# Depthwise taps of a convolution-attention kernel: the second row group's matrix products leave TensorE, and VectorE's taps are placed anew in the first image's dense stage

## Chip, cores and metric

The kernel runs on one core of a Trainium2 chip. The core has a matrix engine (TensorE, PE in the profile, with PEld for its weight loads), VectorE (DVE), ScalarE (ACT), GpSimd (POOL) and SyncE (SP); the last two mainly issue DMAs here. Each engine runs its own instructions in order and waits for others by semaphores. The metric is device time in microseconds (us), the median of several runs. All times inside the program are counted from the start of the profiled execution's span.

## What is computed

Four images of 384 channels by 48x48 pixels go through one layer. It has a depthwise 7x7 convolution (49 taps per channel) whose normalised result is added to the queries of an eight-head attention over 2304 tokens, an output projection and a residual:

```python
local = lax.conv_general_dilated(x, conv_w, window_strides=(1, 1), padding='SAME',
    dimension_numbers=('NCHW', 'OIHW', 'NCHW'), feature_group_count=C)
local = local * inv[None, :, None, None] + (bn_beta - bn_mean * inv)[None, :, None, None]
x_norm = _layernorm(x_flat, ln_gamma, ln_beta)
qkv = x_norm @ qkv_w.T + qkv_b
local_q = _layernorm(local_flat, ln_gamma, ln_beta)
q = q + local_q
attn = jax.nn.softmax(jnp.einsum('bhnd,bhmd->bhnm', q, k) * scale, axis=-1)
out = x_flat + (attn @ v) @ proj_w.T + proj_b
```

## The kernel before

**Tiles.** Channels lie on 128 partitions in three chunks. An image's 48 rows are cut into five row groups of 8, 10, 10, 10 and 10 rows (384 or 480 columns). The code counts these over all images as t = 0 to 19. Keys and values are made by six column groups of 384 tokens (g = 0 to 5).

**Dense stage of the first image.** Group g = 0 is made first, then a loop runs over g = 1 to 5 (inside the main function, after `making = from_x(0, 0)`). For each g, `from_x` yields projections on TensorE (line L568): values, keys, queries. Between its steps the loop writes the layer norm of the next group: `mean_by_chunk` (TensorE), `centre` (VectorE, L489), `squares` (ScalarE), `mean_by_chunk` of the squares, `root` (ScalarE), `newton` and `scale` (VectorE, L505, L506, L563). The scaled group is what the next group's projections read. `lows_out(n)` writes n low halves of keys on VectorE (L661) and sends keys out by DMA (`keys_out`): pair 0 on SP into the key stacks, the others on GpSimd into a DRAM tile `wide`. In the last pass (g = 5) the norm is that of row group 0's convolution, and it ends in `query_end(0)`, `high_queries(0, 0)` and `low_queries(0, 0)`. Those make the first pair's queries; `low_queries` ends in six DMAs on SP (L830, L832), which stack them for the score matmuls.

**Attention slots.** After that each row group has 12 slots: pairs of heads p = 0 to 3 times three thirds of the keys. A slot has six score tiles (L952, each followed by an exponential on ScalarE, L960) and then six weighing steps (L967). The tile `pt` that an exponential writes is shared, four buffers in all, with the dense stage's key tiles `k`, so it waits for their DMAs. At a pair's second slot `high_queries` (ScalarE) and `low_queries` (VectorE, L825, then SP's DMAs) make the next pair's queries. For the first four row groups of an image, the next row group's convolution is normalised by means on TensorE: for row group 0 after its slot 8 TensorE takes the mean of row group 1's sums, so it needs all of their taps.

**Taps.** `conv_ops(t)` yields one VectorE instruction per tap and chunk (L307; the first tap of a chunk L303), 147 in all per row group, into the sums `acc`. Taps are ordered by distance from the centre and go over the chunks in turn. For the first two row groups some taps of chunk 0 are done on TensorE instead: `products` multiplies the slab of pixels by diagonal matrices made on ScalarE. Row group 0 has 10 such taps (`PE_TAPS`), row group 1 has 18 (`MORE_TAPS`); the remaining taps of chunk 0 then come after all those of chunks 1 and 2. The 18 diagonals are made by `make_more` (L335) in two `qs` buffers, and the products are issued after the dense loop, as the last work of TensorE before slot 0; ScalarE writes their sum to the accumulator (L1105).

**Where taps run.** In the dense stage `convolve_first(n)` issues the next n taps at the place where it stands. From slot 0 on `convolve(point)` issues a share. `plan` fixes the shares before anything runs: each half slot has an estimated spare VectorE time (`room`), each row group's convolution has a place by which it is due (`due`), and the taps at a place are its room times the highest rate that any of the coming due places asks for.

**Order.** On PE, VectorE and ScalarE the order is that of the code. The order of the DMA issues on SP and GpSimd is chosen by a scheduler.

Of the kernel before, what the change touches and what calls it, by code (L numbers as in the profile page):

```python
# [10 lines left out]
F32 = mybir.dt.float32  # L11
HALF = mybir.dt.float32r
AF = mybir.ActivationFunctionType
# [3 lines left out]
P = 128  # L17
# [12 lines left out]
OUT_SLOT = 7  # L30
WARM = 14
PE_TAPS = 10
MORE_TAPS = 18

# [11 lines left out]
def unshifted_pass(  # L48
# [16 lines left out]
    nc = tc.nc  # L65
# [3 lines left out]
    CC = C // P  # L69
# [10 lines left out]
    GM = max(ROWS) * W  # L80
# [5 lines left out]
    def size(a):  # L86
        return a.stop - a.start

    def columns_of(t):
        return size(tokens[t % NA])  # L90
# [3 lines left out]
    work = ctx.enter_context(tc.tile_pool(name="work", bufs=2))  # L94
# [5 lines left out]
    def two_banks(name="r"):  # L100
        return ps.tile([P, 2, 512], F32, tag="r", name=name)
# [19 lines left out]
    slabs = {}  # L121

    def load_slab(b, g, parts=1, queue=nc.gpsimd):
        first, end = max(0, row_of[g] - PAD), min(H, row_of[g + 1] + PAD)
        t = work.tile([P, CC, GM + 2 * PAD * W], F32, tag="slab", name=f"slab{b}_{g}")

        edges = (first, row_of[g + 1], end) if parts == 2 else (first, end)
        for a, e in zip(edges, edges[1:]):
            load_packed(t[:, :, (a - first) * W : (e - first) * W], x[b, :, a * W : e * W], queue)
        slabs[b, g] = (t, first, end)  # L130
# [15 lines left out]
    cw, shift = vec[:, :, 0:T0], vec[:, :, T0]  # L146
# [7 lines left out]
    ident = const.tile([P, P], F32, tag="ident", name="ident")  # L154
# [46 lines left out]
    for c in range(CC):  # L201
        for r, n, first in ((0, HD, 0), (64, HD, 1), (48, 16, 6), (112, 16, 7)):
            head = first + 2 * c if first < 6 else first
            ch = head * HD + (16 * c if first >= 6 else 0)
            while n:
                part = min(n, P - ch % P)
                pieces.append((c, r, ch // P, ch % P, part))
                r, n, ch = r + part, n - part, ch + part
# [56 lines left out]
    taps = sorted(range(KS * KS), key=lambda t: (abs(t // KS - PAD), abs(t % KS - PAD)))  # L265
    accs = {}

    def window(slab, a, g, first, end, c, tap):

        dy, dx = tap // KS - PAD, tap % KS - PAD  # L270
        r0, r1 = max(row_of[g], -dy), min(row_of[g + 1], H - dy)
        c0, c1 = max(0, -dx), min(W, W - dx)
        if r0 >= r1:
            return None
        img = slab[:, c, : (end - first) * W].rearrange("p (h w) -> p h w", w=W)
        a = a.rearrange("p (h w) -> p h w", w=W)
        return (
            img[:, r0 + dy - first : r1 + dy - first, c0 + dx : c1 + dx],
            a[:, r0 - row_of[g] : r1 - row_of[g], c0:c1],
        )  # L280

    def conv_ops(t):
        b, g = divmod(t, NA)
        if t + 1 < NT:
            load_slab(*divmod(t + 1, NA))
        slab, first, end = slabs[b, g]
        acc = work.tile([P, CC, GM], F32, tag="acc", name=f"acc{t}", bufs=3)[:, :, : columns_of(t)]
        accs[t] = acc
        if t == 0:
            nc.vector.memset(acc[:, 0, :], 0.0)  # L290

        order = [(tap, c) for tap in taps for c in range(CC)]
        if t < 2:
            mine = [(tap, 0) for tap in taps[(PE_TAPS, MORE_TAPS)[t] :]]
            order = [o for o in order if o[1]] + mine
        for tap, c in order:
            part = window(slab, acc[:, c, :], g, first, end, c, tap)
            if not part:
                continue
            src, dst = part  # L300
            weight = cw[:, c, tap : tap + 1]
            if tap == taps[0]:
                nc.vector.tensor_scalar(  # L303
                    dst, src, weight, shift[:, c : c + 1], ALU.mult, ALU.add
                )
            else:
                nc.vector.scalar_tensor_tensor(dst, src, weight, dst, ALU.mult, ALU.add)  # L307
            yield

    def diagonal(i):  # L310
        return diagonals[i // 6].rearrange("p i f -> p (i f)")[:, i % 6 * P : i % 6 * P + P]
# [2 lines left out]
        for i in range(PE_TAPS):  # L314
            nc.scalar.mul(diagonal(i), ident, cw[:, 0, taps[i] : taps[i] + 1])

    def products(g, n, diagonal):
        total = two_banks()[:, 0, : columns_of(g)]
        slab, first, end = slabs[0, g]
        for i, tap in enumerate(taps[:n]):  # L320
            src, part = window(slab, total, g, first, end, 0, tap)
            nc.tensor.matmul(part, lhsT=diagonal(i), rhs=src, start=i == 0, stop=i == n - 1)  # L322
        return total

    more = []

    def more_diagonal(i):
        return more[i // 9][:, i % 9 * P : i % 9 * P + P]

    def make_more():  # L330
        for tag, bufs in (("qs", 5), ("qs", 5)):
            d = work.tile([P, CC, GM], F32, tag=tag, name="more", bufs=bufs)
            more.append(d.rearrange("p c g -> p (c g)"))
            for i in range(9 * len(more) - 9, 9 * len(more)):
                nc.scalar.mul(more_diagonal(i), ident, cw[:, 0, taps[i] : taps[i] + 1])  # L335
            yield

# [41 lines left out]
            (5, 1): 4.5, (5, 2): 0.6,  # L381
        }.get((g, h), 0.0)

    points, room = [], []
    for t in range(NT):
        if t % NA == 0 and t:
            points += [("kv", t, g, h) for g in range(NG) for h in range(5)]
# [3 lines left out]
    each = CC * KS * KS  # L391
    due = []
    counts = [0]
    weights = [0.0]
    for t in range(1, NT):
        last = ("slot", t - 1, norm_slots(t - 1)[0] - (t >= NA), t < NA) if t % NA else ("kv", t, 4, 0)
        counts.append(t * each - MORE_TAPS)
        weights.append(weights[-1] + (counts[-1] - counts[-2]) * columns_of(t) / G)
        due.append((points.index(last), weights[-1]))
    share = {}  # L400
# [6 lines left out]
    def plan(done):  # L407

        given = done
        done = done * columns_of(1) / G  # L410
        for i, point in enumerate(points):
            ahead = [(sum(room[i:end]), n - done) for end, n in due if end > i]
            rate = max((n / time for time, n in ahead[: 2 * NA]), default=0.0)
            done += rate * room[i]
            share[point] = taps_in_all(done) - given
            given = taps_in_all(done)
        assert given == counts[-1]

    def convolve(*point):
        for _ in range(share[point]):  # L420
            next(stream)
# [6 lines left out]
    class Norm:  # L428
# [34 lines left out]
        def sum(self):  # L463
            self.add(self.src)
# [239 lines left out]
    def lows_out(n):  # L704
        for _ in range(n):
            lows.popleft()()
# [63 lines left out]
    def key_bias(m):  # L770
        nc.vector.tensor_add(qkb[:, 1, :], qk_vec[:, 1, :], m[1])
        nc.vector.tensor_add(vbp[:, :, 0], vbp[:, :, 0], m[2])

    def query_bias(m):

        nc.vector.tensor_add(qkb[:, 0, :], qk_vec[:, 0, :], m[0])
        nc.vector.tensor_add(qkb[:, 0, :], qkb[:, 0, :], beta)
# [218 lines left out]
    def convolve_first(n):  # L996
        nonlocal n_first
        n_first += n
        for _ in range(n):
            next(stream)  # L1000
# [36 lines left out]
    next(making)  # L1037
    for c in range(CC):
        scale_rows(0, c)
    first_sum = products(0, PE_TAPS, diagonal)  # L1040
    m, bank = columns()
    convolve_first(10)
    norm = Norm(xn[0, 1])
    norm.mean_by_chunk(norm.src, bank)
    convolve_first(12)
    key_bias(m)
    query_bias(m)
    next(making)
    norm.centre()
# [9 lines left out]
    norm.scale(norm.newton())  # L1059
    both(making)  # L1060
    convolve_first(7)
    making_more = make_more()
    for g in range(1, NG):

        last = g == NG - 1
        next(making_more, None)
        making = from_x(0, g)
        both(making)
        assert not last or n_first >= each - PE_TAPS
        norm = Norm(accs[0] if last else xn[0, g + 1])  # L1070
        norm.mean_by_chunk(norm.src)
        if last:
            added = output_bias()
        if g in (3, 5):
            keep_stack(0, g // 2 - 1)
        convolve_first(4)
        norm.centre()
        norm.squares()
        both(making)
        if not last:  # L1080
            convolve_first(4)
            both(making)
        norm.mean_by_chunk(norm.buf)
        norm.root()
        lows_out(1)
        if last:
            both(making)
        both(making)
        convolve_first(6 if last else 10)
        if not last:  # L1090
            lows_out(2)
        if last:
            local_end(0, norm.newton())
        else:
            norm.scale(norm.newton())
        next(making)
        if last:
            query_end(0)
            high_queries(0, 0)
            low_queries(0, 0)  # L1100
        next(making)
        if not last:
            convolve_first(7)
    lows_out(2)
    nc.scalar.activation(  # L1105
        accs[1][:, 0, :], products(1, MORE_TAPS, more_diagonal), AF.Identity, bias=shift[:, 0:1]
    )
    nc.vector.tensor_add(pb, pb, added)
    plan(n_first - (each - PE_TAPS))

    for t in range(NT):
        b, g = divmod(t, NA)
# [71 lines left out]
        first, second = norm_slots(t)  # L1184
        for s in range(NSLOT):
            pair, part = divmod(s, KB // BATCH)
# [90 lines left out]
    for i, at in enumerate(pieces_out):  # L1277
        ao, n = aos[i], size(at)
# [555 lines left out]
```

## Time and profile before

| what | value |
|---|---|
| median of 4 runs | 2785.94 us (2783.3 to 2787.38) |
| the profiled execution's own time | 2785.26 us |
| its span, first to last instruction | 2783.5 us |
| PE busy | 2750.2 us (99%) |
| DVE busy | 2340.1 us (84%) |
| ACT busy | 1639.5 us (59%) |
| POOL busy | 696.1 us (25%) |
| taps on VectorE, L307, 2854 instructions | 1679.5 us |
| products with diagonals of row group 1, L322, on the chain | 14.05 us, from 158.31 us |
| first score matmul | 172.29 us |
| mean granted TensorE clock | 0.996 of full speed |

A busy engine in the profile is not necessarily one at full speed, since the ends of matmuls are modelled. A row of a timeline gives start, length, engine, line, operation, output and inputs, shapes and count; the bracket at its end is the engine's idle time before it and what ended that.

### The profile page before, as it was taken

How to read it: one execution, taken by the hardware profiler on the slowest of the kernel's cores; microseconds unless marked ns; L12 is line 12 of the kernel's file. 1: busy time of each engine (PE TensorE's matmuls, PEld its weight loads, DVE VectorE, ACT ScalarE, POOL GpSimd, SP SyncE). 2: the span in 40 equal slices, each digit the busy share in tenths (PEclk: the TensorE clock that was granted, in tenths of full speed). 3: DMA queues.
4: the chain of work that ended last, by engine and by line, in shares of the span. 5: the costliest groups of instructions: out<-in, count | busy, mean ns of one | idle time of the engine just before them, and what ended most of it. 6: DMA issues, size and time to landing. Idle time of an engine off the chain costs nothing.

```text
span 2783.5 us, 46399 instructions
## 1 busy us (share of the span) xinstructions
PE 2750.2 (99%) x16438; PEld 1556.8 (56%) x16438; DVE 2340.1 (84%) x4082; ACT 1639.5 (59%) x2281; POOL 696.1 (25%) x1273
## 2 busy tenths in 40 slices
PE   9998999999999999999999999999999999999999
PEld 6565555555555655555556565555555565555555
DVE  6879999989999999989888999898889889987112
ACT  4345666666423766767632577677652276676662
POOL 5731111111375111110257311101117701110110
PEclk9999999999999999999999999999999999999999
DMA  7344444445455454454635554545546545444442
GB/s 142 98 113 122 121 123 131 121 127 134 126 165 151 130 140 129 129 143 124 167 104 153 151 145 127 126 126 148 135 121 167 128 141 133 138 125 137 141 145 75
DMA packets 163298, 369.15 MB, mean 133 GB/s; under 512 B 61488, under 2 KB 112208, under 8 KB 163056
## 3 DMA queue, kind: packets, MB, share of 16 engines
q0 software_dynamic: 76992, 284.75, 35.9%
q1 hardware_dynamic: 83072, 77.72, 12.3%
q10 hardware_dynamic: 2992, 3.62, 0.4%
q8 instruction: 132, 2.16, 0.3%
q14 instruction: 110, 0.90, 0.1%
HBM read 258.14 MB, written 64.14 MB: 116 GB/s over the span
## 4 chain that ended last, share of the span: by engine, by line
PE 88%; DVE 7%; POOL 2%; DMA 2%; ACT 1%; issue 1%; SPq 0%; DVEq 0%; ACTq 0%; POOLq 0%
PE o L967 39%; PE r L952 31%; PE r L568 16%; DVE acc L307 5%; DMA wide<-k 1%; PE r L322 1%; POOL wide L594 1%; DMA slab<-in_x_dram 1%; POOL wide L619 0%; POOL wide L592 0%; POOL wide L591 0%; POOL wide L613 0%; DMA qs<-qs 0%; DVE k L661 0%; PE r L1010 0%
## 5 line engine op out<-in xcount | busy, mean ns | idle before, releaser
L307 DVE SCALAR_TENSOR_TENSOR acc<-slab,vec,acc 128x450 f32<-128x450 f32 (+8 forms) x2854 | 1679.5, 657 | 2.2
L960 ACT ACTIVATE pt<-r 128x960 f32<-128x960 f32 (+1 forms) x1440 | 1248.5, 943 | 237.6 <-PE o L967 150.0
L967 PE MATMUL o<-pt,v 128*64 128x480 f32 (+1 forms) x5760 | 1169.7, 556 | 5.6 <-ACT pt L960 5.6
L952 PE MATMUL r<-qs,ks 64*128 64x480 f32 (+1 forms) x8640 | 969.3, 373 | 9.6 <-DMA qs<-qs 6.4
L952 PEld LDWEIGHTS r<-qs,ks 64*128 64x128 f32 x8640 | 784.0, 184 | 276.9 <-issue 167.9
L967 PEld LDWEIGHTS o<-pt,v 128*64 128x64 f32 x5760 | 394.2, 137 | 665.9 <-issue 584.7
L628 POOL DMA_DIRECT2D ks<-wide x228 | 165.5, 726 | 1363.5 <-PE r L952 1323.1
L568 PE MATMUL r<-xn,w_qk 128*128 128x384 f32 x864 | 283.7, 486 | 0.0
L849 ACT COPY o<-o 113x480 f32<-113x480 f32 (+1 forms) x160 | 87.1, 544 | 299.4 <-PE o L967 299.4
L568 PEld LDWEIGHTS r<-xn,w_qk 128*128 128x128 f32 x864 | 164.3, 190 | 114.3
L868 DVE TENSOR_TENSOR ao<-ao,o 113x480 f32<-113x480 f32 (+1 forms) x120 | 76.1, 634 | 97.1 <-ACT o L849 97.0
L568 PE MATMUL r<-w_v,xn 128*128 128x384 f32 x432 | 144.7, 487 | 0.0
L650 ACT COPY v<-r 128x384 f32<-128x384 f32 x72 | 32.1, 480 | 188.4 <-PE r L568 188.4
L568 PEld LDWEIGHTS r<-w_v,xn 128*128 128x128 f32 x432 | 81.6, 190 | 58.1 <-issue 2.9
L594 POOL DMA_DIRECT2D wide<-k x192 | 96.5, 507 | 10.4 <-issue 7.4
L619 POOL DMA_DIRECT2D wide<-k x192 | 93.0, 489 | 0.1
L859 ACT COPY ao<-o 113x480 f32<-113x480 f32 (+1 forms) x60 | 32.7, 545 | 102.1 <-PE o L967 102.1
L613 POOL DMA_DIRECT2D wide<-k x144 | 71.7, 500 | 77.4 <-ACT k L658 60.6
L825 DVE TENSOR_TENSOR qs<-xn,qs 128x480 fp32r<-128x480 f32 (+1 forms) x60 | 38.0, 633 | 57.4 <-ACT qs L820 57.3
L108 POOL DMA_DIRECT2D slab<-in_x_dram x76 | 47.1, 626 | 155.0 <-DVE acc L307 154.7
L568 PE MATMUL r<-af,w_o 128*128 128x384 f32 (+1 forms) x270 | 85.2, 470 | 0.0
L675 ACT ACTIVATE xn<-r,qkb 128x384 f32<-128x384 f32 x72 | 41.2, 578 | 67.4 <-PE r L568 65.6
(139 smaller groups left out, 1349.2 us busy)
## 6 DMA issues: line engine op xcount, KB each, us to landing
ks<-wide POOLq DMA_DIRECT2D x228, 768.0 KB, 5.2
qs<-qs SPq DMA_DIRECT2D x352, 60.0 KB
wide<-k POOLq DMA_DIRECT2D x480, 24.0 KB, 1.9
slab<-in_x_dram POOLq DMA_DIRECT2D x24, 432.0 KB, 7.2
wide<-k POOLq DMA_DIRECT2D x192, 48.0 KB, 1.9
wide<-ks POOLq DMA_DIRECT2D x12, 768.0 KB, 4.2
xr<-in_x_dram POOLq DMA_DIRECT2D x16, 576.0 KB, 5.5
rb<-rden SPq DMA_DIRECT2D x32, 270.0 KB
```

What stands on the lines that cost most here:

```text
L108: queue.dma_start(out=dst[p0 : p0 + piece.shape[0]], in_=piece)
L307: nc.vector.scalar_tensor_tensor(dst, src, weight, dst, ALU.mult, ALU.add)
L568: nc.tensor.matmul(dst, lhsT=weights(c), rhs=src(c), start=c == 0, stop=c == CC - 1)
L594: queue.dma_start(out=dst[r + 32 * i : r + 32 * i + 32, 1], in_=k[r + 16 : r + HD, 1])
L613: nc.gpsimd.dma_start(out=last[16 * u : 16 * u + 16, 0], in_=k[r : r + 16, 0])
L619: nc.gpsimd.dma_start(out=last[to : to + 16, 1], in_=k[r : r + 16, 1])
L628: nc.gpsimd.dma_start(out=place_keys(b, p, i), in_=wide[b, p][:, :, at])
L849: nc.scalar.copy(part[0 : 64 + HA], sums[0 : 64 + HA, 0, :n])
L868: nc.vector.tensor_add(dst, dst, part[0 : 64 + HA])
L952: nc.tensor.matmul(r[:, j, :n], lhsT=ks[rows, w, at], rhs=qs[rows, m, :], start=i == 0, stop=i == 2,)
L960: nc.scalar.activation(pt, r[:, :, :n], AF.Exp, scale=SCALE)
L967: nc.tensor.matmul(sums[halves[j], 0, : columns_of(t)], lhsT=values[t // NA, kb // NB][:, first : first + 64], rhs=pt[:, j, :], start=i == ...
```

## The change

`MORE_TAPS` and everything that served it go: the 18 products of row group 1, the two tiles of diagonals with their 18 ScalarE instructions, and the ScalarE copy of the sum. Row group 1 is convolved wholly on VectorE, its 147 taps in the common order over three chunks. In the dense stage the numbers of taps at the places change: 46 instead of 37 ahead of the loop, 32 instead of 25 in each of the passes g = 1 to 4, 21 instead of 10 in the last pass, which has a new place behind `root`. The planner gets a new place, `("start",)`, with a room of 14.0 us ahead of slot 0, and its share is issued there.

```diff
-MORE_TAPS = 18
+FIRST_ROOM = 14.0
...
-        if t < 2:
-            mine = [(tap, 0) for tap in taps[(PE_TAPS, MORE_TAPS)[t] :]]
-            order = [o for o in order if o[1]] + mine
+        if t == 0:
+            order = [o for o in order if o[1]] + [(tap, 0) for tap in taps[PE_TAPS:]]
...
-    def make_more():
-        for tag, bufs in (("qs", 5), ("qs", 5)):
-            d = work.tile([P, CC, GM], F32, tag=tag, name="more", bufs=bufs)
-            more.append(d.rearrange("p c g -> p (c g)"))
-            for i in range(9 * len(more) - 9, 9 * len(more)):
-                nc.scalar.mul(more_diagonal(i), ident, cw[:, 0, taps[i] : taps[i] + 1])
-            yield
...
-    points, room = [], []
+    points, room = [("start",)], [FIRST_ROOM]
...
-        counts.append(t * each - MORE_TAPS)
+        counts.append(t * each)
...
     norm.mean_by_chunk(norm.src, bank)
-    convolve_first(12)
+    convolve_first(18)
     key_bias(m)
+    convolve_first(3)
     query_bias(m)
...
     for g in range(1, NG):
...
-        next(making_more, None)
...
-        convolve_first(4)
+        convolve_first(8)
         norm.centre()
         norm.squares()
         both(making)
         if not last:
-            convolve_first(4)
+            convolve_first(7)
             both(making)
         norm.mean_by_chunk(norm.buf)
         norm.root()
+        if last:
+            convolve_first(9)
         lows_out(1)
...
-        convolve_first(6 if last else 10)
+        convolve_first(4 if last else 10)
...
     lows_out(2)
-    nc.scalar.activation(
-        accs[1][:, 0, :], products(1, MORE_TAPS, more_diagonal), AF.Identity, bias=shift[:, 0:1]
-    )
     nc.vector.tensor_add(pb, pb, added)
     plan(n_first - (each - PE_TAPS))
+    convolve("start")
```

More of the change, by code (lines that the diff above doesn't have):

```diff
@@ L315, in make_diagonals, with products @@
             nc.scalar.mul(diagonal(i), ident, cw[:, 0, taps[i] : taps[i] + 1])
[L317 to L322, printed above, removed]
-        return total
-    more = []
-    def more_diagonal(i):
-        return more[i // 9][:, i % 9 * P : i % 9 * P + P]
-    def make_more():
-        for tag, bufs in (("qs", 5), ("qs", 5)):
-            d = work.tile([P, CC, GM], F32, tag=tag, name="more", bufs=bufs)
-            more.append(d.rearrange("p c g -> p (c g)"))
-            for i in range(9 * len(more) - 9, 9 * len(more)):
-                nc.scalar.mul(more_diagonal(i), ident, cw[:, 0, taps[i] : taps[i] + 1])
-            yield
+    def products():
+        total = two_banks()[:, 0, : columns_of(0)]
+        slab, first, end = slabs[0, 0]
+        for i, tap in enumerate(taps[:PE_TAPS]):
+            src, part = window(slab, total, 0, first, end, 0, tap)
+            nc.tensor.matmul(
+                part, lhsT=diagonal(i), rhs=src, start=i == 0, stop=i == PE_TAPS - 1
+            )
+        return total
     def norm_slots(t):
@@ L1039, in unshifted_pass @@
         scale_rows(0, c)
-    first_sum = products(0, PE_TAPS, diagonal)
+    first_sum = products()
     m, bank = columns()
@@ L1061, in unshifted_pass @@
     convolve_first(7)
-    making_more = make_more()
     for g in range(1, NG):
         last = g == NG - 1
-        next(making_more, None)
         making = from_x(0, g)
```

## The prediction

> **What bounds the kernel now.** The change touches only the first image, so I read the chain of waits up to 380 us first. It shows TensorE without a gap through the dense stage, then row group 1's products, then slot 0:
>
> ```profile
> 36.13 122.18 PE r L568 x390
> 158.31 14.05 PE r L322 x36
> 172.36 3.35 PE r L952 x36
> ```
>
> Next TensorE's timeline over the first row group's slots, whose idle times are in the brackets:
>
> ```profile
> 235.56 4.09 PE L967 MATMUL o<-pt,v 128*64 128x384 f32 x24
> 247.50 5.14 PE L568 MATMUL r<-acc,mean_w 128*128 128x480 f32 x6 [7.85 <-DVE acc L307]
> ...
> 281.63 4.18 PE L952 MATMUL r<-qs,ks 64*128 64x480 f32 x35 [2.17 <-DMA qs<-qs]
> ```
>
> After slot 8 TensorE waits 7.85 us for row group 1's last tap, and the six matmuls then take 5.14 us where the same shape takes 2.68 at 260.14 us. The windows by stage show why, in the clock column (0.74):
>
> ```profile
> 240.00:260.00 20.00, 12.50 (x66) 6.78 (x66) 19.38 (x31) 6.57 (x11) 3.79 (x6) 0.74 0.56 120
> ```
>
> So VectorE's taps cost 7.85 + 2.46 = 10.3 us here. VectorE's own timeline tells where it could have worked earlier:
>
> ```profile
> 77.00 1.35 DVE L489 TENSOR_TENSOR xn<-xn,r 128x1152 f32<-128x1152 f32 x1 [2.28 <-PE r L568]
> ...
> 81.86 0.62 DVE L661 SCALAR_TENSOR_TENSOR k<-r,qkb,k 128x384 fp32r<-128x384 f32 x1 [1.49 <-ACT k L658]
> ...
> 131.86 0.61 DVE L505 SCALAR_TENSOR_TENSOR sq<-r,eps,sq 128x384 f32<-128x384 f32 x1
> ...
> 147.73 0.62 DVE L661 SCALAR_TENSOR_TENSOR k<-r,qkb,k 128x384 fp32r<-128x384 f32 x1 [5.52 <-DMA slab<-in_x_dram]
> ...
> 157.75 12.99 DVE L307 SCALAR_TENSOR_TENSOR acc<-slab,vec,acc 128x450 f32<-128x450 f32 x21
> 180.71 0.56 DVE L825 TENSOR_TENSOR qs<-xn,qs 128x384 fp32r<-128x384 f32 x1 [9.98 <-ACT qs L820]
> ```
>
> It idles some 4 us a pass up to g = 3, less at g = 4, 5.52 in the last pass and 9.98 before slot 1's queries.
>
> **Removed.** 14.05 us of TensorE. ScalarE's 18 diagonals (5.5 us busy) and one copy (0.66 us) lie beside idle time of ScalarE and are worth nothing.
>
> **Added to VectorE.** 18 taps, but the remaining ones get cheaper. The same shapes cost less when neighbours write different chunks:
>
> ```profile
> 199.26 8.57 DVE L307 SCALAR_TENSOR_TENSOR acc<-slab,vec,acc 128x460 f32<-128x460 f32 x14
> ...
> 237.84 9.51 DVE L307 SCALAR_TENSOR_TENSOR acc<-slab,vec,acc 128x480 f32<-128x480 f32 x13
> ```
>
> 8.57/14 = 0.61 us with two chunks in turn, 9.51/13 = 0.73 with chunk 0 alone. Before: 98 x 0.61 + 31 x 0.73 = 82.4 us; after: 147 x 0.61 = 89.7, so +7.3 us. [...]
>
> **The dense stage gets longer.** A pass takes TensorE 21.28 us (L489 waited for it at 55.72, 77.00 and 98.28). VectorE's fixed work per pass is 1.27 (L489) + 3 x 0.53 (L661) + 2.52 (L505, L506, L563) = 5.4 us, which leaves 15.9 for taps. After the change 32 lie between one pass's L505 and the next's. Adding up the start-to-start steps of the same taps where they now stand (row group 1's at 0.61): taps 72 to 103 take 15.1 us, 104 to 135 (chunk 0 alone) 18.6, 136 to 167 19.3. So VectorE overruns by 2.7 us in g = 3 and 3.4 in g = 4; with 0.5 late at g = 2 its `newton` is 6.6 us late at g = 4. TensorE's next group begins at 70.99 and 21.28-us steps after, 1.25 us behind the end of `scale` (69.74). The rest, 5.3 us, is TensorE's delay, and with 0.2 for late squares in the last pass the stage ends at 163.8 instead of 158.3.
>
> Last pass: `scale` of g = 4 ends at 140.1; 15 taps 9.2, centre 1.4, 9 taps 5.5, one low 0.5, 4 taps 2.4, `newton` to `query_end` 4.2, `low_queries` 0.6: 163.8 (156.7 before), the two lows at 164.3 and 164.8.
>
> **Slot 0: the cover is gone.** The 14 us also hid what comes behind `low_queries`: SP's six DMAs and the key DMAs on GpSimd, which must land before the third exponential may overwrite a shared `pt` buffer. The second image's start, which has no products, shows both waits (TensorE, then ScalarE):
>
> ```profile
> 878.25 3.82 PE L952 MATMUL r<-qs,ks 64*128 64x384 f32 x35 [1.43 <-DMA qs<-qs]
> 884.01 5.79 PE L967 MATMUL o<-pt,v 128*64 128x384 f32 x24 [1.94 <-ACT pt L960]
> ```
> ```profile
> 883.06 0.81 ACT L960 ACTIVATE pt<-r 128x768 f32<-128x768 f32 x1 [2.17 <-DMA wide<-k]
> ```
>
> There the exponential came 9.1 us after the second low (873.97). In the first image's own rows GpSimd issued that tile's last DMA at 163.4 after a low at 157.2, plus 0.5 to issue and 2.0 to land, less 0.5 for an issue that moves ahead: 8.2 us. So the third exponential starts at 172.5 to 173.9, weighing 0.95 later, lasting 4.1 or (as at 884.01) 5.8 us. Slot 1 starts at 177.4 to 180.6, against 179.67 before. I take 179.0: of the 14 us removed, 0.7 is left.
>
> The Trainium skill, TensorE: Matmul & The Clock Gate, section "Why this matters for your kernels", speaks against the change: TensorE idle for more than about 3 us falls back to half clock. Between 163.8 and the queries' landing it would idle some 4 us; by the rule one window of about 3.4 us at half rate, 1.7 us, most of it under the wait for the exponential. The row at 884.01 has the same 1.7 us after 1.43 and 1.94 us of idling, the row at 281.63 nothing after 2.17.
>
> **Ahead of slot 0, and a new wait.** By the planner's arithmetic the start gets 24 taps, row group 0's slots 123 (153 before). Pair 1's `low_queries` now stands behind 24 + 16 taps: 164.9 + 24.5 + 0.6 = 190.0. Behind it wait SP's four DMAs, and TensorE's slot 3. From such a low to its scores took 6.8 us (274.79 to 281.63, one key load beside it) and 9.5 us (208.30 to 217.84, image loads too); the first is nearer, I take 7: 197.0. Undisturbed, slot 3 would start at 179.0 + 2 x 7.38 = 193.8; TensorE waits 3.2 us. Pair 2: 33 taps 20.2 and three short instructions 1.4 later, 211.6, landed at 218.6 to 221.1, against slot 6 at 197.0 + 22.1 = 219.1: 1 us more, 220.1 (217.84 before). Pair 3 is free of it (233 against 242). Row group 1's last tap ends 16 taps later, 222; TensorE asks at 220.1 + 22.1 = 242.2. The 7.85 and the 2.46 are gone: the mean ends at 244.9 instead of 252.56, 7.7 us. One tap fewer ahead of `low_queries(1, 0)` gives 0.6 of the 2.17, the earlier taps 0.2 at 354.55; half clock after the new waits takes 0.5 back. Sum 8 us. From 380 us on TensorE hardly waits and the plan nearly repeats, so it is kept: 2785.26 - 8 = 2777.3, and 2778 beside the median, which lies 0.7 above the profiled execution.
>
> **Rivals.** *Full gain:* the taps fit the waits, the queries land in time: 14.05 + 10.3 = 24, so 2762. For it: the idle brackets. Against it: 18.6 and 19.3 us of taps in 15.9 of room, and the second image's start. Chance 0.08. *Moved, not paid:* the waits at slots 3 and 6 eat what slot 8 gave (9.5 us each to land and half clock after each, with key loads in front): 2783, no change that a measurement of this kernel can tell (0.2%, 5.6 us). For it: the row at 217.84. Chance 0.18. *Slower:* VectorE becomes the bound of the slots. If a tap there takes 0.73 instead of 0.61, pair 1's low comes 4.8 us later, each later pair's 4.0 more, slot 6 at 230 and row group 1's scores at 283; with half clock after three waits 5 more: 288, so 2792. It decides from about 0.73 us a tap. For it: the rows of chunk 0 alone; against: three chunks in turn. Chance 0.12. That the debt only moves to row group 2 I exclude: at its due place 306 of 294 taps are issued.
>
> **Numbers.** The forecast has 0.62, with its own range from 2772 (queries land in 4.5 us: no wait at slots 3 and 6, none of the 2.17) to 2781 (180.6, 9.5 us, 1.7 us of clock: gain 5). 2768 to 2786 holds 8 in 10. Faster: 0.57 of the forecast plus 0.08, with 0.02 of the middle case, 0.67; same 0.21; slower 0.12.
>
> **What would show it.** L505 of the later passes follows L661 without idle time, and TensorE shows gaps of 2 and 3.4 us ahead of the groups g = 4 and 5; the dense stage ends near 163.8, the first weighing starts at 173 to 175; `qs<-qs` holds slot 3 for about 3 us; the mean after slot 8 has no VectorE wait and takes 2.7 us. Wrong, if the passes stay at 21.28 us, or if slot 1 starts more than 3 us away from 179.

## Result, and the profile after

| | median | runs |
|---|---|---|
| before | 2784.67 us (2780.77 to 2790.3) | 60 |
| after | 2781.78 us (2777.2 to 2785.66) | 40 |
| ratio | 0.9988, 95% interval 0.9984 to 0.9993 | |

The change gains 2.9 us: the interval leaves out 1, but the gain is inside the 0.2% that the prediction counts as no change. The time is 3.8 us above the forecast, a little outside the forecast's own range (2772 to 2781) and inside the wide one (2768 to 2786). Two later sets of runs of the changed kernel gave 2779.53 us (0.9981, 0.9972 to 0.999) and 2780.68 us (0.9991, 0.9982 to 1.0).

The profiled execution of the changed kernel took 2777.99 us, with a span of 2776.2 us. TensorE's timeline of it (start, length, engine, line, operation, output and inputs, shapes, count, and the idle time before with its releaser in brackets):

```profile
116.76 4.14 PE L556 MATMUL r<-w_v,xn 128*128 128x384 f32 x12 [1.71 <-DVE xn L551]
...
141.24 5.80 PE L556 MATMUL r<-w_v,xn 128*128 128x384 f32 x12 [2.93 <-DVE xn L551]
...
156.63 9.84 PE L556 MATMUL r<-xn,w_qk 128*128 128x384 f32 x30
167.49 0.41 PE L940 MATMUL r<-qs,ks 64*128 64x384 f32 x1 [1.02 <-DMA qs<-qs]
169.02 3.40 PE L940 MATMUL r<-qs,ks 64*128 64x384 f32 x35 [1.12 <-DMA qs<-qs]
173.99 4.11 PE L955 MATMUL o<-pt,v 128*64 128x384 f32 x24 [1.57 <-ACT pt L948]
...
196.03 4.99 PE L940 MATMUL r<-qs,ks 64*128 64x384 f32 x36 [3.17 <-DMA qs<-qs]
...
221.73 3.04 PE L940 MATMUL r<-qs,ks 64*128 64x384 f32 x31 [1.23 <-DMA qs<-qs]
...
243.48 2.68 PE L556 MATMUL r<-acc,mean_w 128*128 128x480 f32 x6
...
275.10 4.17 PE L940 MATMUL r<-qs,ks 64*128 64x480 f32 x35 [2.30 <-DMA qs<-qs]
```

The wait of 7.85 us in front of the mean is gone (243.48 has no bracket and takes 2.68 us). In its place stand small new ones: two in the dense stage (116.76, 141.24), three around slot 0, one at slot 3 (196.03) and one at slot 6 (221.73). Two rows are also long for their shape: the 12 value matmuls take 5.80 us at 141.24 and 4.14 at 116.76, and slot 3's scores take 4.99 us where undisturbed ones take 3.42. The windows by stage show the granted clock in the third column from the right:

```profile
138.50:148.50 10.00, 7.26 (x18) 4.18 (x19) 9.93 (x17) 1.29 (x3) 9.91 (x21) 0.83 0.31 77
195.00:202.00 7.00, 5.97 (x44) 5.22 (x46) 7.00 (x12) 3.21 (x5) 0.68 (x1) 0.76 0.01 3
240.00:260.00 20.00, 18.95 (x125) 10.65 (x120) 13.09 (x20) 12.65 (x20) 1.28 (x2) 1.00 0.25 81
```

The half-clock stretch behind slot 8 (0.74 before) is gone, and two have appeared, at 141 and 196 us, where TensorE now idles. VectorE's timeline shows who keeps slots 3 and 6 waiting:

```profile
165.68 24.57 DVE L306 SCALAR_TENSOR_TENSOR acc<-slab,vec,acc 128x450 f32<-128x450 f32 x40
190.16 0.55 DVE L813 TENSOR_TENSOR qs<-xn,qs 128x384 fp32r<-128x384 f32 x1
...
211.83 0.55 DVE L813 TENSOR_TENSOR qs<-xn,qs 128x384 fp32r<-128x384 f32 x1
...
222.38 1.40 DVE L302 TENSOR_SCALAR acc<-slab,vec 128x480 f32<-128x480 f32 x3
```

40 taps, 24 of them the portion ahead of slot 0, run before pair 1's low queries (190.16); pair 2's come at 211.83. Row group 1's last tap ends at 222.4 (row group 2's first begins there), 21 us ahead of its mean: the taps are now early, and the queries behind them late. The chain of waits follows slot 6 back (start, length, what):

```profile
211.90 0.47 DVE qs L813
...
215.03 6.57 DMA qs<-qs
221.60 0.14 issue
221.73 3.04 PE r L940 x31
```

From pair 2's low queries to the scores that need them it is 9.9 us, 6.57 of them one transfer. So by this reading slot 6 starts when VectorE says so, and what TensorE loses ahead of it costs nothing more; the experiment that fills the idle time, further on, bears this out.

**One measure for all traces.** How early row group 0's ten products start differs between executions of one kernel (28.59, 29.48 and 29.93 us in three traces of the kernel before; 29.92, 29.99 and 27.79 in three of the changed one), as the first loads land. So in what follows, *M* is the end of row group 1's mean less the start of those products: 247.50 + 5.14 - 28.59 = 224.0 before, 243.48 + 2.68 - 29.92 = 216.2 after.

### The profile page after: what moved, and what is told of

Its sections match the earlier page's. It is cut to its first block, busy times and chain, and to the rows that moved or that the text cites. A ratio compares the mean times of both kernels' runs of the same rounds, so it can differ in the third digit from the quotient of the medians.

```text
span 2776.2 us, 46317 instructions
## 1 busy us (share of the span) xinstructions
PE 2735.1 (99%) x16402; PEld 1550.4 (56%) x16402; DVE 2347.9 (85%) x4100; ACT 1632.8 (59%) x2262; POOL 695.8 (25%) x1273
## 4 chain that ended last, share of the span: by engine, by line
PE 85%; DVE 6%; DMA 4%; POOL 3%; ACT 1%; issue 1%; SPq 0%; DVEq 0%; ACTq 0%; POOLq 0%
PE o L955 40%; PE r L940 33%; PE r L556 12%; DVE acc L306 4%; DMA wide<-k 1%; POOL wide L582 1%; DMA slab<-in_x_dram 1%; DMA qs<-qs 1%; POOL wide L607 1%; DMA staged<-in_qkv_wT_dram 0%; DVE k L649 0%; POOL wide L580 0%; POOL wide L579 0%; DMA ks<-k 0%; POOL wide L601 0%
## 5 line engine op out<-in xcount | busy, mean ns | idle before, releaser
L306 DVE SCALAR_TENSOR_TENSOR acc<-slab,vec,acc 128x470 f32<-128x470 f32 (+9 forms) x2871 | 1687.6, 656 | 1.2
```

## The experiments

All medians of one set of runs share the runs of the kernel before (2783.6 to 2784.7 us).

| variant | median us | ratio to before, 95% | M us |
|---|---|---|---|
| changed, first trace | 2781.78 | 0.9988 (0.9984 to 0.9993) | 216.2 |
| changed, second and third trace | 2779.53, 2780.68 | 0.9981, 0.9991 | 218.4, 216.4 |
| no portion ahead of slot 0 | 2772.99 | 0.9956 (0.9943 to 0.997) | 209.6 |
| dense stage not lengthened | 2775.93 | 0.9967 (0.9955 to 0.9979) | 213.7 |
| both, and 4 taps less in the last pass | 2767.06 | 0.993 (0.9916 to 0.9943) | 204.5 |
| products kept | 2787.89 | 1.0011 (1.0002 to 1.002) | 224.9 |
| products removed, taps as before | 2785.36 | 0.9997 (0.9988 to 1.0006) | 220.0 |
| pair 1's queries first | 2783.61 | 1.0005 (0.9995 to 1.0015) | 220.1 |
| pairs 1 and 2 first | 2779.28 | 0.9982 (0.9973 to 0.9991) | 214.9 |
| idle time filled | 2779.6 | 0.9982 (0.9973 to 0.9991) | 218.9 |
| before, two more traces | one run each | | 223.1, 223.3 |

**Without the portion ahead of slot 0.**

```diff
-FIRST_ROOM = 14.0
+FIRST_ROOM = 0.0
```

> The changed kernel with the portion ahead of slot 0 taken out (24 taps, 14.6 us of VectorE; the slots of row group 0 get 130 taps for 123). Theory (the early portion holds pair 1's low queries back): the wait of 3.17 us for qs ahead of slot 3, the wait of 1.23 us ahead of slot 6 and the half-clock window of 1.6 us at 195.8 us are gone, row group 1's taps still end before its mean asks for them; the mean of row group 1 ends 4 to 6 us earlier than in the changed kernel, time about 2777. Rival (the portion is needed: without it the taps end too late): the mean after slot 8 waits for VectorE by 2 us or more, time 2781 to 2784. Second rival (what is missing is lost elsewhere in the run): the waits go, the time stays at 2781 to 2782.

VectorE's timeline, and the mean on TensorE's, of this kernel:

```profile
176.85 0.56 DVE L813 TENSOR_TENSOR qs<-xn,qs 128x384 fp32r<-128x384 f32 x1 [2.60 <-ACT qs L808]
...
199.60 0.56 DVE L813 TENSOR_TENSOR qs<-xn,qs 128x384 fp32r<-128x384 f32 x1
...
224.00 1.43 DVE L302 TENSOR_SCALAR acc<-slab,vec 128x480 f32<-128x480 f32 x3
```
```profile
234.82 2.68 PE L556 MATMUL r<-acc,mean_w 128*128 128x480 f32 x6
```

Pair 1's low queries come 13 us earlier, pair 2's 12 (2.0 of it because its products start that much sooner), and slots 3 and 6 have no wait. Row group 1's last tap still ends at 224.0 us, 11 us ahead of its mean. M falls by 7 to 9 us and the time to 2773, more than the theory gave: the portion was the dearest part of the change. It bought nothing, since nothing was short of taps.

**With the dense stage not lengthened.** The 11 taps go to the slots.

```diff
-        convolve_first(8)
+        convolve_first(4 if g in (3, 4) else 8)
...
-            convolve_first(7)
+            convolve_first(4 if g == 4 else 7)
```

> The changed kernel with 11 taps fewer in the dense stage (4 fewer ahead of the centring of passes 3 and 4, 3 fewer behind the squares of pass 4), which go to the slots. Theory (passes 3 and 4 are lengthened by VectorE, and the idle time there costs a half-clock window besides): the waits of 1.71 and 2.93 us for xn and the window at 141.2 us go, the dense stage ends at 159 to 160.5 us for 166.5, and slot 1 starts 6 to 7 us earlier (171 to 172 us); pair 1's low queries move with it, so the wait ahead of slot 3 stays at about 3 us. Time about 2775 to 2777. Rival (the time of the dense stage is given back later, as taps that are missing at slot 8 or in a longer wait at slot 3): slot 1 earlier, but the end of row group 1's mean where it was (245 to 247 us), time 2780 to 2782.

TensorE's timeline of this kernel (it has no idle time ahead of the value matmuls any more):

```profile
161.21 0.41 PE L940 MATMUL r<-qs,ks 64*128 64x384 f32 x1 [2.90 <-DMA qs<-qs]
...
189.16 5.21 PE L940 MATMUL r<-qs,ks 64*128 64x384 f32 x36 [2.04 <-DMA qs<-qs]
...
216.18 4.19 PE L940 MATMUL r<-qs,ks 64*128 64x384 f32 x31 [2.33 <-DMA qs<-qs]
```

The dense stage ends at 158.3 us, as before the change. The waits at slots 3 and 6 stay, since the portion stays, and both their rows run partly at half clock (5.21 us for 3.42, 4.19 for 3.04), but M is 2.5 to 4.7 us less. The theory's time holds (2775.93).

**The products kept**, with the diagonals, the 18 taps taken off VectorE, and the new tap counts and the portion as in the changed kernel:

```diff
+    nc.scalar.activation(
+        accs[1][:, 0, :], products(1, MORE_TAPS, more_diagonal), AF.Identity, bias=shift[:, 0:1]
+    )
     nc.vector.tensor_add(pb, pb, added)
```

> The changed kernel with the 18 products of row group 1 put back (and their diagonals), and the tap counts of the dense stage and the portion ahead of slot 0 kept. Theory (the products are 14 us of TensorE's chain, of which some cover work that the first slots wait for): scores start at 180 to 181 us for 167.5, slot 1 some 11 us later than in the changed kernel, the wait ahead of slot 3 gone (3.2 us and its half-clock window of 1.6), so the mean of row group 1 ends 5 to 7 us later; time 2786 to 2789, no better than the kernel before. Rival (the gain came from the placing of the taps, and the products were cover): mean of row group 1 within 2 us of the changed kernel's, time 2781 to 2783.

TensorE's timeline of it:

```profile
164.82 14.21 PE L323 MATMUL r<-slab,more 128*128 128x480 f32 x36
178.97 3.42 PE L952 MATMUL r<-qs,ks 64*128 64x384 f32 x36
...
227.25 4.29 PE L952 MATMUL r<-qs,ks 64*128 64x384 f32 x31 [2.22 <-DMA qs<-qs]
...
250.51 2.68 PE L568 MATMUL r<-acc,mean_w 128*128 128x480 f32 x6
```

Slot 0 has no wait here: the 14.21 us cover the landing of its queries and keys, and the portion, and slot 3 has none either. Slot 6 still waits for pair 2's queries (2.22 us in the last of its waits). M is 224.9, 6.5 to 8.7 us later than in the changed kernel: of the products' 14 us 5 to 8 were cover. The theory's time holds (2787.89) and the rival falls: the new placing of the taps without the removal is no gain (1.0011).

**The products removed and nothing else**: the tap counts of the kernel before, no portion.

> The products gone, but the tap counts of the dense stage as in the kernel before and nothing ahead of slot 0. Theory (the products alone are no gain, since VectorE's taps decide): scores start at about 160 us, row group 1's 137 taps that are left take VectorE to 248 to 250 us, TensorE waits 12 us or more for them behind slot 8, and the mean ends at 250 to 253 us for 252.6; time within 2 us of the kernel before, 2783 to 2786. Rival (the products' 14 us are gain by themselves): the wait behind slot 8 stays at about 8 us and the time falls to 2774 to 2778.

TensorE's timeline of it:

```profile
211.61 6.39 PE L940 MATMUL r<-qs,ks 64*128 64x384 f32 x35 [3.01 <-DMA qs<-qs]
...
244.36 4.86 PE L556 MATMUL r<-acc,mean_w 128*128 128x480 f32 x6 [7.52 <-DVE acc L306]
```

The time is that of the kernel before, as expected (0.9997). The wait for the taps is 7.5 us and not 12, because slot 6 takes 3.01 us and two half-clock windows first. M is 3.1 to 4.0 us below that of the kernel before, which the time does not show: what one trace gains by the mean can be lost further on. Neither half of the change, as it is made here, is worth anything alone: the removal needs the taps placed, and the placing needs the removal.

**The changed kernel again**, for a second trace and more times.

> The changed kernel itself once more, for a second trace and for its times beside the other variants. Theory (its new waits of 1 to 3 us in the first 280 us are caught, or not, by the half-clock windows of 3.4 us, and the first trace was a lucky one with two of them up to 275 us): time 2781 to 2783, and in this trace three or four windows up to 280 us where the first had two ahead of slot 11, or as many, with a time near 2778. Rival (the first trace is typical): two windows at the same two places, and a time over 2780 all the same, with the difference elsewhere in the run.

**And a third time**, beside the filler further on.

> The changed kernel itself, beside the one with the filler, for its times on the same chip and a third trace. By both theories 2779 to 2783; a window at 141 us, and one or two more between slots 3 and 6.

TensorE's timeline of the second and then of the third trace, at the places of the waits in the dense stage and at slots 3 and 6:

```profile
141.33 5.71 PE L556 MATMUL r<-w_v,xn 128*128 128x384 f32 x12 [2.93 <-DVE xn L551]
194.29 3.65 PE L940 MATMUL r<-qs,ks 64*128 64x384 f32 x36 [1.58 <-DMA qs<-qs]
...
221.89 5.13 PE L940 MATMUL r<-qs,ks 64*128 64x384 f32 x31 [2.66 <-DMA qs<-qs]
```
```profile
139.12 4.11 PE L556 MATMUL r<-w_v,xn 128*128 128x384 f32 x12 [2.93 <-DVE xn L551]
...
195.47 5.19 PE L940 MATMUL r<-qs,ks 64*128 64x384 f32 x36 [4.15 <-DMA qs<-qs]
```

The same wait of 2.93 us is followed by 5.71 us of value matmuls in one execution and by 4.11 in the other. By the clock's records half clock comes in windows of 3.4 us, and an idle time meets one or not: it can't be booked from one trace. Between 100 and 280 us the first trace has two such windows (141.2, 195.8 us), the second four (141.2, 219.7 a double one, 277.7), the third four (165.0 a double one, 195.8, 274.3). So the theory is right about the number of windows, and the first trace was a lucky one in this; but the third has none at 141 us, where one was expected, and the medians are 2779.53 and 2780.68, a little below the first set's. The first of them is below what either theory or rival expected (2781 to 2783, over 2780), the second within its 2779 to 2783.

**Both repairs together.** As the two edits above, with the last pass's four taps gone too.

```diff
-        convolve_first(4 if last else 10)
+        convolve_first(0 if last else 10)
```

> Both repairs together: no portion ahead of slot 0, the 11 taps less in passes 3 and 4, and the last pass's 4 taps ahead of its Newton step left out too; all of them go to the slots (138 taps in row group 0's). Theory (the two losses are separate and add up, and the slots have the room): no wait for xn in the dense stage, scores start at 158 to 160 us, no wait of over 1.5 us at slots 3 and 6, row group 1's taps end some 2 us ahead of its mean; time 2764 to 2767. Rival (VectorE is now the bound of the slots): the mean after slot 8 waits for VectorE, or slot 6 for its keys behind pair 2's low queries, by 3 us or more; time 2769 to 2772.

TensorE's timeline of it:

```profile
160.06 0.41 PE L940 MATMUL r<-qs,ks 64*128 64x384 f32 x1 [0.46 <-DMA qs<-qs]
161.53 0.63 PE L940 MATMUL r<-qs,ks 64*128 64x384 f32 x4 [1.05 <-DMA qs<-qs]
...
231.55 2.68 PE L556 MATMUL r<-acc,mean_w 128*128 128x480 f32 x6
```

Nothing waits between slot 1 and the mean. The theory's time holds but for 0.06: 2767.06 us (5 runs, 2761.56 to 2770.56), 16.5 us below the kernel before in the same set and 12 to 15 below the changed one. Against the changed kernel the two repairs alone gave 8.8 and 5.9 us by their medians, 14.7 together: they add up, though the last pass's four taps went too and were not tried alone. This version beats both kernels.

**Pair 1's queries ahead of the portion**, which stays.

```diff
+    for p in range(1, 2):
+        high_queries(0, p)
+        low_queries(0, p)
     convolve("start")
...
-            if part == 1 and pair < NP - 1:
+            if part == 1 and pair < NP - 1 and (t or pair >= 1):
```

> The changed kernel with pair 1's high and low queries put ahead of the portion of 24 taps, nothing else moved. Theory (the portion makes VectorE late for everything behind it: the wait at slot 6 ends with a key load that stands on GpSimd's queue behind a load into xn, which waits for pair 2's low queries on VectorE, at 211.8 us in the changed kernel): the 3.17 us ahead of slot 3 go, slot 6 waits some 5 to 6 us for 1.23, the mean of row group 1 ends within 2 us of the changed kernel's; time 2779 to 2782. Rival (only the order of pair 1's queries and the taps was wrong): slot 3 and slot 6 without a wait over 1.5 us; time 2774 to 2778.

TensorE's timeline at slot 6:

```profile
214.13 0.41 PE L940 MATMUL r<-qs,ks 64*128 64x384 f32 x1 [1.61 <-DMA qs<-qs]
218.00 1.00 PE L940 MATMUL r<-qs,ks 64*128 64x384 f32 x4 [3.46 <-DMA qs<-qs]
221.30 4.75 PE L940 MATMUL r<-qs,ks 64*128 64x384 f32 x31 [2.30 <-DMA qs<-qs]
```

Slot 3 no longer waits, and slot 6 waits 7.4 us instead, with three half-clock windows: the debt is handed on, not paid. The theory is right in this and the rival falls, but its numbers don't hold: slot 6 waits 7.4 us and not 5 to 6, M is 1.7 to 3.9 us above the changed kernel's, and 2783.61 us is above its 2779 to 2782. Its text also names the wrong releaser. It is the queries' own transfer (6.84 us in the chain of waits, 214.33 to 221.17); the chain holds no key load. The loads into xn and the key load behind them are released by the same low queries and run beside that transfer; a transfer of a pair's queries took 2.57 us at slot 0 in the next variant; that they slow it down is argued, not shown.

**Pairs 1 and 2 ahead of the portion.** As before, with `range(1, 3)` and `pair >= 2`.

> As the kernel before it, with pair 2's high and low queries ahead of the portion as well, so that neither pair 1's nor pair 2's wait for taps, and GpSimd's load into xn finds its buffer free. Theory (order, not the number of taps): no wait over 1.5 us at slots 3 and 6, the mean of row group 1 asked for some 5 us earlier, its taps (done at 222 us) still ahead of it; time 2774 to 2777, near the kernel without the portion. Rival (the early portion costs by VectorE's load as such, whatever the order): waits of 3 us or more at other places, time 2779 to 2782.

GpSimd's timeline, then TensorE's at slot 8:

```profile
222.20 1.14 POOL L108 DMA_DIRECT2D slab<-in_x_dram x1 [19.91 <-DVE acc L306]
223.33 0.72 POOL L616 DMA_DIRECT2D ks<-wide x1
```
```profile
230.78 4.97 PE L940 MATMUL r<-qs,ks 64*128 64x384 f32 x36 [3.37 <-DMA ks<-wide]
```

Slots 3 and 6 are free, and slot 8 waits 3.37 us for its keys: their load stands on GpSimd's queue behind a slab load, which waits 19.91 us for row group 1's last tap to leave the buffer. So order repairs two waits, and the load of VectorE shows at a third. This is the rival, by its wait at another place and by its time (2779 to 2782, here 2779.28): no better than the changed kernel.

**Idle time filled.** 33 products of 128x128 that nothing reads, in the waits.

```diff
+            if b == 0 and blk == 0:
+                fill(r[:, :P], {4: 7, 5: 12}.get(g, 0))
             project(
...
+        if t == 0 and p == 1 and kb == 0:
+            fill(r[:, 0, :P], 14)
```

> The changed kernel with idle TensorE time filled by products that nothing reads, 128x128 at some 0.21 us each, written to the tile that the next real product overwrites: 7 ahead of pass 4's values (1.71 us of wait in the changed kernel), 12 ahead of pass 5's (2.93 us), 14 ahead of slot 3's scores (3.17 us). No wait is shortened by them. Theory (the half-clock windows follow TensorE's idle time, and cost up to 1.7 us each on top of the waits): no window at about 141 us nor at slot 3; the mean granted clock of its runs higher than the changed kernel's by 0.0005 to 0.001; 2 to 3.5 us faster than the changed kernel in the same set of runs. Rival (the windows come of themselves and have nothing to do with those waits): windows and time as in the changed kernel, within 1 us, or a little more for the filler.

TensorE's timeline of it:

```profile
138.66 4.04 PE L556 MATMUL r<-w_v,xn 128*128 128x384 f32 x12
...
190.75 3.39 PE L620 MATMUL r<-ident,mean_w 128*128 128x128 f32 x28
194.07 3.42 PE L948 MATMUL r<-qs,ks 64*128 64x384 f32 x36
...
220.07 4.58 PE L948 MATMUL r<-qs,ks 64*128 64x384 f32 x31 [2.60 <-DMA qs<-qs]
```

The value matmuls and slot 3 run at full clock, and over the 11 runs of each kernel the mean granted clock is 0.9963, for 0.9945 of the changed kernel beside it and 0.9964 of the kernel before. So the half-clock windows follow these waits. The time gains only 1.1 us by the medians, with intervals that overlap, and not the 2 to 3.5 of the theory: what is won ahead of slot 6 is waited for there (2.60 us). Pair 2's low queries, which slot 6 waits for, come 181.9 us behind row group 0's products in both kernels (211.83 - 29.92 in the changed one, 209.08 - 27.14 here), so VectorE sets slot 6. Half clock is a companion of these waits, and filling them is no cure.

**The kernel before, two more traces.**

> The kernel before, for a second trace of it. What is asked: three traces of the changed kernel end row group 1's mean 216.2, 218.3 and 216.3 us behind the first of row group 0's ten products with diagonals, the one trace of the kernel before 224.0, a gain of 5.7 to 7.8 us, and yet the medians differ by 3 to 5 us. Theory (the one trace of before is on the late side, by the half-clock stretch of 10.2 us behind the wait at slot 8): 221 to 223 us here. Rival (it is typical, and the gain is lost again at the later images' starts): 224 us within 0.5.

> The kernel before, for a third trace; as for the one before it.

The mean behind slot 8 in these two, from TensorE's timeline:

```profile
248.40 4.19 PE L568 MATMUL r<-acc,mean_w 128*128 128x480 f32 x6 [7.89 <-DVE acc L307]
```
```profile
248.85 4.34 PE L568 MATMUL r<-acc,mean_w 128*128 128x480 f32 x6 [8.01 <-DVE acc L307]
```

M is 223.1 and 223.3, between the two texts (221 to 223, and 223.5 to 224.5) and nearer the first: the first trace was late by 0.8 to 0.9 us, from the half clock (5.14 us for these six, here 4.19 and 4.34); the wait itself is steady (7.85, 7.89, 8.01).

## Why the prediction was too good, step by step

**Held.** The path to the mean, nearly term by term:

| step | forecast | first trace, with the 1.33 us by which its products start later |
|---|---|---|
| gaps ahead of g = 4, 5 | 2 and 3.4 us | 1.71 and 2.93 |
| dense stage ends | 163.8 | 166.47: 165.1, of which 1.7 is half clock |
| first weighing | 173 to 175 | 173.99: 172.7 |
| slot 1 starts | 179.0 | 178.03: 176.7 |
| wait at slot 3 | 3.2 us | 3.17 |
| wait at slot 6 | 1 us | 1.23 |
| last tap of row group 1 | 222 | 222.4: 221.1 |
| mean ends | 244.9 | 246.16: 244.8 |

40 taps took 24.57 us, 0.61 each, so the rival of the slots bound by 0.73 us a tap falls. The mean's wait of 7.85 us went, and in the first trace the end of the mean is 7.8 us earlier in M, for 7.7 forecast. That the two agree so well is in part luck: slot 1 started 2.3 us ahead of the forecast, and half clock at slot 3 cost 1.6 us that the forecast did not have there. On the mean of three traces of each kernel M falls from 223.5 to 217.0, by 6.5 us. That the products were cover was right too: slot 1 comes 3 us sooner than before (the forecast left 0.7), and with the products kept M is 6.5 to 8.7 us later, not 14.

**Failed.** The path was right and the sum of 8 us too large. Part of it is in the clock's terms: "The 7.85 and the 2.46 are gone" and "half clock after the new waits takes 0.5 back". The 2.46 is one trace's; the other two of the kernel before show 4.19 - 2.68 = 1.5 and 4.34 - 2.68 = 1.7. The new waits' half clock cost TensorE 5.80 - 4.11 = 1.7 and 4.99 - 3.42 = 1.6 in the first trace, 3.3 and not 0.5. But what TensorE loses ahead of slot 6 is not added to the time there: slot 6's weighing starts 194.8 us behind the products in the first trace and 194.9 in the third, which has a window more ahead of it. In the second it starts at 197.0, since there two windows fall on slot 6's own scores (5.13 us for 3.04).

Another part is in "it is kept" from 380 us on. Counted from the products, row group 1's slot 1 is 6.6 us earlier on the mean of three traces each and the last slot of the run 5.8, but in between some 2 us are lost at the second image's start and half of that comes back: the weighing of the first image's last slot is 6.7 us earlier, of the second image's second slot 4.8, of the third image's second slot 5.8. TensorE's timeline of the first trace at the second image's first slot:

```profile
872.83 0.66 PE L940 MATMUL r<-qs,ks 64*128 64x384 f32 x1 [3.20 <-issue]
874.16 5.38 PE L940 MATMUL r<-qs,ks 64*128 64x384 f32 x35 [0.67 <-DMA qs<-qs]
```

The waits in this slot are 3.87, 5.60 and 2.94 us in the three traces of the changed kernel and 3.37, 2.98 and 3.23 before, and half clock holds for 6.8 us in each of the three, for 3.4, none and 3.4 before. At the third image's start it is the other way round: one window of 3.4 us in each trace before, none after. Why the second image starts worse is not shown.

**Also off, and smaller.** The "0.6 of the 2.17" did not come: that wait is 2.30, 2.70 and 2.38 us in the three traces (2.17, 2.68 and 2.50 before). That no half clock follows it (4.18 us at 281.63) is the first trace's too: in the other two of the kernel before these scores take 5.75 and 5.98 us. And the base moved: the median of the kernel before was 2785.94 us over 4 runs, 2784.67 over 60.

**Open.** The traced gain of 5.8 us is above the runs' 2.9 (4.1 and 3.2 in the two later sets). The three traced executions of the kernel before took 2785.26, 2784.84 and 2789.3 us, none below its median, so some of it can be chance. Over the runs the mean granted clock of the changed kernel is 0.9949, 0.9956 and 0.9945 in its three sets, that of the kernel before 0.9963 to 0.9966 in the sets run with the variants: 0.0010 to 0.0018 of 2780 us, 2.8 to 5 us of TensorE's time, where the forecast had the clock gaining 2. That is the size of what is missing between 8 and 2.9, but it is not shown to be the cause: the filler brought the clock back to 0.9963 for 1.1 us of time, and the traced executions do not have the difference (0.996, 0.995 and 0.995 before, 0.997, 0.995 and 0.995 after).

**The rivals.** The measured time lies beside *moved, not paid* (2783), which had its mechanism right in one place: from pair 2's low queries to slot 6's scores it took 9.9 us, nearly the 9.5 it used. What kept the change from *full gain* (2762) was for the most part two placings that the working had priced and took as given: the lengthened passes and the portion. Without them the kernel comes to 2767.06.

## What to carry to other kernels

An order given to one engine's queue is paid by what stands behind it: before filling an engine's idle time, list what else that engine owes in the next slots (here the low queries), and leave the filler out where nothing is short of it. Placed behind two pairs' queries it did not pay either: the wait came back at a third place. When the work that is placed ends 21 us before it is needed, the placing is too early, and the margin is the first thing to give back. And idle times of 1 to 3 us on TensorE should be priced over several traces as the wait plus some 1.7 us for each half-clock window behind it, and only where no other engine sets the next start: two windows fell on slot 6's scores in the second trace of the changed kernel (5.13 us for 3.04).

## What was not expected of the hardware

Half clock follows idle times shorter than 3 us, and not always: after 2.93 us in two traces of the changed kernel out of three (5.80 and 5.71 us for 4.11), after 1.54 and 2.66 us close together in the second trace of the changed kernel. The Trainium skill, TensorE: Matmul & The Clock Gate, section "Why this matters for your kernels", asks for no idle gap above some 3 us; these rows show a half-clock window after less.

The last transfer of a pair's low queries took 2.57 us at slot 0 in the variant with pairs 1 and 2 first and 6.57 us at slot 6 of the changed kernel, where GpSimd issued loads of 72 to 768 KB in the same 3 us; that they are the reason is not shown.
